# Windowed gated attention with a mixing layer behind it: maxima three patches ahead instead of four, residual tiles and mixed rows stored from ScalarE's queue

## The chip, the cores and the metric

One core of a Trainium2 chip runs the whole program. The metric is device time in microseconds of one execution, and the number that is compared is the median of several runs. A core has five engines with one in-order instruction queue each: TensorE (PE, with its weight loads as PEld), VectorE (DVE), ScalarE (ACT), GpSimd (POOL) and SyncE (SP). SP does no arithmetic here; it issues transfers between DRAM and the on-chip memory. Any instruction that waits for a semaphore holds everything behind it in its own queue.

## The reference

The input x is 8 batches of 512 rows and 2048 columns. Two layers are added to it. Both normalise each row first.

```python
x = x + tanh(g_x) * xattn(layernorm(x), ctx, mask)   # attention in windows
x = x + tanh(g_f) * ffn(layernorm(x))                # four streams, mixed

def xattn(qk, v, masks):            # 16 patches of 128 columns a batch
    q, k = Wq @ patches(qk) + bq, Wk @ patches(qk) + bk      # 256 x 128
    val = Wv @ patches(v) + bv
    scores = q_head.T @ k_head / sqrt(32)                    # 8 heads
    o = gelu(softmax(mask(scores)) @ val_head)
    return masks * (Wo @ o + bo)

def ffn(x):                         # x as 512 rows of 4 streams x 512
    xn = x * rsqrt(mean(x * x) + eps)
    H_res = sinkhorn(xn @ W_res.T + base, 50 iterations)     # 4 x 4 a row
    H_pre, H_post = softmax(xn @ W_pre.T + ..), softmax(xn @ W_post.T + ..)
    H = (1 - g) * I + g * H_res
    y = (H_pre-weighted sum of the streams) @ W_branch
    return H @ streams + H_post * y
```

## The kernel before

**Tiling.** A block is 512 columns (BLK), so a batch has 4 blocks and the run 32 blocks n, each of 4 patches t = 4n + p of 128 columns. A half is 256 columns, two patches. The main loop goes over patches, and in each step runs the letters of a string, ORDER, each of which emits one piece of work. Each piece has a priority. A scheduler then places the instructions in one order per engine, by priority and by its own picture of when their inputs are ready. So the order on the engines is not the order of the text, and a change of one piece moves many others.

**The attention's pieces.** `load_x` (L233) loads a block of x three blocks ahead, as two tiles `xt` of 128 x 2 x 512 numbers, from a pool of 10 such buffers. `proj(n)` normalises it, multiplies it in half-precision parts by the weights of q and k (L287 to L289), copies the result out of the accumulators as high and low halves (`ev`, L293 on ScalarE, L294 on VectorE), and SP stores these to DRAM (`qd`, L295). `stack(m)` loads one half back, rearranged by heads, into one of three buffers `QK` (L307, L312; L317 adds a mask row). A buffer is free again when `expo` of the half three before is done with it. `smax(t)` multiplies q by k for a patch (L345), VectorE takes the maxima (L348), TensorE transposes them (L353), ScalarE copies them (`mh`, L355), and SP stores them as rows 97 and 98 of the same QK buffer (L358). `expo(t)` multiplies again with these rows in (L632), so that the maxima are subtracted, and takes the exponential (L634). `attv` applies it to the values, which `vproj` made (L335, copied out at L336), and `outp(n)` applies gelu and mask, multiplies by Wo (L704 to L707), adds the result to x in place in the tile `xt` (L708, VectorE), sums squares of it for the next normalisation (`junk`, L710, ScalarE, which then reads the sum out), and stores the tile to a DRAM copy of the first layer's result, `x1s` (L711, SP). The four row tiles of a block are c = 0 to 3; c = 0, 1 are the two halves of one buffer, c = 2, 3 of the other.

The string has `P` (stacking) ahead of `s` (maxima) in one step. `AHEAD` says how many patches ahead of the current step the maxima are taken. With p = 2, `P` stacks the late half of the next block and `s` takes the maxima of patch t + AHEAD; with p = 3, `p` ends the projection of the block after next and stacks its first half.

**The mixing's pieces.** When a batch's attention is done, `ffn` computes its mixing matrices (the 50 Sinkhorn iterations are a long chain between GpSimd and VectorE, L881 to L891). Then each of its four row tiles is mixed from x1s, either by `mixv`, on VectorE, ScalarE and GpSimd (loads at L952, stores at L991), or by `mixp`, on TensorE: loads `xc` at L1008 into tiles of the xt pool, ScalarE at L1010, TensorE at L1011 (xpp), L942 to L944, L1045 and L1046 (mx), ScalarE at L1048 (`wp`), and a store by SP for each of four groups at L1049. `mixp` takes 12 of the 32 row tiles, all of batches 4 to 7, and nearly all of it runs after the attention is done.

Transfers signal their landing on eight semaphores that are used in turn, over both issuing queues. So a transfer also waits until the one before it on its semaphore has landed, unless another wait covers that.

Of the kernel before, what the change touches and what calls it, by code (L numbers as in the profile page):

```python
# [19 lines left out]
P = 128  # L20
# [5 lines left out]
BLK = 512  # L26
# [5 lines left out]
NS = 3  # L32
HI = 1000
XPRE_POOL = lambda b: b < 7
AHEAD = 4
LXP = 1
SK_POOL = lambda b: b < 7
CT_ACT = False
# [34 lines left out]
D_X1 = 0  # L73
# [24 lines left out]
def gated_xattn_mhc_kernel(  # L98
# [21 lines left out]
    V, A, G, T, SY = nc.vector, nc.scalar, nc.gpsimd, nc.tensor, nc.sync  # L120
# [82 lines left out]
    def defer(k, tag, fn):  # L203
        if k == 0:
            fn()
        else:
            late.append([k, fn, tag])
# [16 lines left out]
    x1s = {}  # L224
    G4 = {}
    ob = {}

    def load_x(n):
        b, k = divmod(n, NBLK)
        xtile[n] = []  # L230
        for c in (0, 2):
            t = xp_.tile([P, 2, BLK], F32, tag="xt", name="xt")
            SY.dma_start(t, x[b, c * P : (c + 2) * P, k * BLK : (k + 1) * BLK].rearrange("(c p) s -> p c s", p=P))  # L233
            xtile[n] += [t[:, 0], t[:, 1]]

    EXP_SET = "natural_log_exp_and_others"

# [124 lines left out]
    with tc.tile_pool(name="set", bufs=1) as st:  # L362
# [31 lines left out]
        for n in range(NBLK):  # L394
            load_x(n)
# [263 lines left out]
    def outp(n):  # L659

        b, k = divmod(n, NBLK)
        o = ob.pop(n)
        for g in range(2):
            gi = A.activation(o[:, g], o[:, g], AF.Gelu, bias=bvc[:, g : g + 1])  # L664
        with tc.issue_after(gi.ins), tc.high_priority():
            A.preload_act_table_set(EXP_SET)
        mb = gp.tile([P, BLK], F32, tag="mb", name="mb")
        SY.dma_start(mb, mask[b, k * BLK : (k + 1) * BLK].partition_broadcast(P))
        G.tensor_tensor(o, o, mb.unsqueeze(1).broadcast_to([P, 2, BLK]), ALU.mult)  # L669
        j0 = n * NP  # L670
        gt_ = op_.tile([P, NP, DK + 1], F32, tag="gT", name="gT")
        G.tensor_copy(gt_[:, :, DK], maskT[:, j0 : j0 + NP])
        yield
        for q in range(2):
            pt = ps_t.tile([P, 2, 2, P], F32, tag="t", name="gTp")
            for j in range(2):
                for e in range(2):
                    T.transpose(pt[:, j, e, :], o[:, e, (2 * q + j) * P : (2 * q + j + 1) * P], ident)
            V.tensor_copy(gt_[:, 2 * q : 2 * q + 2, 0:DK], pt.rearrange("p j e s -> p j (e s)"))
        g4 = ps_t.tile([P, DK + 1], F32, tag="t", name="g4")  # L680
        for p in range(NP):
            T.matmul(g4[32 * p : 32 * p + 32, :], Wm[:, k * NP + p, :], gt_[:, p, :], start=True, stop=True)
        if k == 0:
            g4s = lnp.tile([P, DK + 1], F32, tag="g4s", name="g4s", bufs=2)
            V.tensor_copy(g4s, g4)
            G4[b] = g4s
        else:
            V.tensor_tensor(G4[b], g4, G4[b], ALU.add)
        mr = MR[n % 2]
        SY.dma_start(mr[0:6, :], mrow_d[:, n * BLK : (n + 1) * BLK])  # L690
        gh = gp.tile([P, 2, BLK], F32R, tag="gh", name="gh")
        A.copy(gh, o)
        gl = gp.tile([P, 2, BLK], F32R, tag="gl", name="gl")
        G.tensor_tensor(gl, o, gh.bitcast(F32), ALU.subtract)
        if k == 0:
            sq2[b] = lnp.tile([P, 4, NBLK], F32, tag="sq2", name="sq2")
            x1s[b] = x1d.tile([D, S], F32, tag="x1s", name="x1s")
        xt = xtile.pop(n)
        yield
        for c in range(4):  # L700
            ps = ps_p.tile([P, BLK], F32, tag="p", name="op")
            cs = slice(c * P, (c + 1) * P)
            for e in range(2):
                T.matmul(ps, WoH[:, e, cs], gh[:, e], start=(e == 0), stop=False)  # L704
                T.matmul(ps, WoH[:, e, cs], gl[:, e], start=False, stop=False)  # L705
                T.matmul(ps, WoL[:, e, cs], gh[:, e], start=False, stop=False)
            T.matmul(ps, bo6[:, cs], mr, start=False, stop=True)  # L707
            V.tensor_tensor(xt[c], ps, xt[c], ALU.add)  # L708
            jk = fp.tile([P, BLK], BF16, tag="ph", name="junk2", bufs=BUF_PH)
            A.activation(jk, xt[c], AF.Square, bias=nmean[b][:, c : c + 1], accum_out=sq2[b][:, c, k : k + 1])  # L710
            defer(D_X1, "x1", lambda cs=cs, c=c: SY.dma_start(x1s[b][cs, k * BLK : (k + 1) * BLK], xt[c]))  # L711
            yield

    raws = {}
# [279 lines left out]
    def mixp(b, n, maps, inp=False):  # L994

        E, cst, pre, prc, post, rec, HR = maps
        rows = x1s[b].rearrange("d (j e) -> (d j) e", j=4)
        orow = out[b].rearrange("d (j e) -> (d j) e", j=4)
        PD = f1.tile([P, 4, 32], F32, tag="PD", name="PD", bufs=2)
        G.tensor_tensor(PD, blk.unsqueeze(1).broadcast_to([P, 4, 32]), rec[:, 4 * n : 4 * n + 4, 0:1].broadcast_to([P, 4, 32]), ALU.mult)  # L1000
        xc = []
        xo = xp_.tile([P, 2, 512], F32, tag="xt", name="xo")
        xps = (ps_t if inp else ps_p).tile([P, 512], F32, tag="t" if inp else "p", name="xpp")
        for g in range(4):
            q = 4 * n + g
            if g % 2 == 0:
                t2 = xp_.tile([P, 2, 512], F32, tag="xt", name="xc")
                SY.dma_start(t2, rows[q * P : (q + 2) * P, :].rearrange("(g p) s -> p g s", p=P))  # L1008
            t = t2[:, g % 2]
            A.activation(t, t, AF.Identity, bias=rec[:, q, 1:2])  # L1010
            T.matmul(xps[32 * g : 32 * g + 32, :], PD[:, g, :], t, start=True, stop=True)  # L1011
            xc.append(t)
        xs = xo[:, 0]
        A.copy(xs, xps)
        yield 1
        pt = (ps_t if inp else ps_p).tile([P, 4, P], F32, tag="t" if inp else "p", name="xpT")
        for e in range(4):
            T.transpose(pt[:, e, :], xs[:, e * P : (e + 1) * P], ident)
        y = ps_t.tile([P, 512], F32, tag="t", name="yp")
        if inp:  # L1020
            ph = fp.tile([P, 4, P], F16, tag="ph", name="ph", bufs=BUF_PH)
            pl = fp.tile([P, 4, P], F16, tag="pl", name="pl", bufs=BUF_PH)
        else:
            ph = xhp.tile([P, 4, P], F16, tag="xh", name="phb")
            pl = xhp.tile([P, 4, P], F16, tag="xl", name="plb")
        for r in branch(pt, ph, pl, y):
            yield r
        ys = xo[:, 1]
        A.copy(ys, y)
        yield 1  # L1030
        qh = xtp.tile([P, 2, 512], F32, tag="xTt", name="QD")
        QD = qh[:, 0].rearrange("p (t i) -> p t i", i=4)
        HD = qh[:, 1].rearrange("p (g t i) -> p g t i", g=4, i=4)
        G.tensor_tensor(QD, ident.unsqueeze(2).broadcast_to([P, P, 4]), post[:, n, :].unsqueeze(1).broadcast_to([P, P, 4]), ALU.mult)
        G.tensor_tensor(
            HD,
            blk.unsqueeze(1).unsqueeze(3).broadcast_to([P, 4, 32, 4]),
            HR[:, 4 * n : 4 * n + 4, :].unsqueeze(2).broadcast_to([P, 4, 32, 4]),
            ALU.mult,
        )  # L1040
        pw = None if inp else [ps_s.tile([P, 2, 512], F32, tag="s", name="mx") for _ in range(2)]
        for g in range(4):
            q = 4 * n + g
            ps = ps_t.tile([P, 512], F32, tag="t", name="mx1") if inp else pw[g // 2][:, g % 2]
            T.matmul(ps, QD[:, 32 * g : 32 * g + 32].rearrange("p t i -> p (t i)"), ys, start=True, stop=False)  # L1045
            T.matmul(ps, HD[:, g].rearrange("p t i -> p (t i)"), xc[g], start=False, stop=True)  # L1046
            w = fp.tile([P, 512], F32, tag="w", name="w", bufs=BUF_W) if inp else ep.tile([P, 512], F32, tag="eh" if g % 2 else "e32", name="wp", bufs=1 if g % 2 else BUF_EP)
            A.activation(w, ps, AF.Identity, bias=rec[:, q, 2:3])  # L1048
            SY.dma_start(orow[q * P : (q + 1) * P, :], w)  # L1049
            yield 1  # L1050

    NT_ = NTOT * NP
# [5 lines left out]

    for t in range(2, AHEAD):
        smax(t)  # L1060
    def at(name, fn, *args):

        p0 = tc.cur_priority
        tc.cur_priority = p0 + PRI[name]
        r = fn(*args)
        tc.cur_priority = p0 + tc.cur_priority - p0 - PRI[name]
        return r
# [15 lines left out]
    def act(c, t):  # L1083
# [20 lines left out]
        elif c == "l" and live_:  # L1104
            if p == LXP and n > 1 and n + 3 < NTOT:
                load_x(n + 3)
        elif c == "s" and live_ and t + AHEAD < NT_:
            at("smax", smax, t + AHEAD)
        elif c == "v" and live_:
# [119 lines left out]
```

## Time and profile before

| | us |
|---|---|
| three runs: median (lowest to highest) | 1695.94 (1693.8 to 1705.01) |
| profiled execution: time, span | 1699.8, 1698.0 |
| TensorE busy 141 to 567 / 567 to 992 / 992 to 1418 / 1513 to 1698 us | 398.1 of 426 / 377.9 of 425 / 357.9 of 426 / 160.5 of 185 |
| VectorE busy in the same | 242.2 / 331.9 / 332.2 / 123.1 |
| ScalarE busy in the same | 274.6 / 298.8 / 281.2 / 90.4 |
| DMA engines' mean busy share in the same | 0.77 / 0.71 / 0.63 / 0.46 |

The span runs from the first instruction to the last; the profiled execution's own time is 1.8 us longer. In this execution the mean granted TensorE clock is 0.954 of full speed. Up to about 141 us the weights are prepared and the first blocks projected; from 567 us on, attention and mixing of earlier batches run side by side; the last residual tile is stored at 1513 us, and from there to the end there is only the Sinkhorn chain of the last batches and mixing.

How to read it: a group line of the page names line, engine, operation, output and inputs with their shapes, and count; then busy time, mean duration in ns, and the idle time of the engine just before these instructions with what ended it. A line of waits says which engine stood before which line and for whom, in us in total, times, and the longest. SPq is SP's queue: it has no busy time, but its waits show what was held. The chain is the sequence of work that ended last, followed back from the end. The ends of matmuls are modelled, so a busy TensorE is not a TensorE at its peak.

Of the issues, the x1s stores are 128 of 256 KB and the mixed rows' stores (`wp`) 48 of 256 KB, all on SP; ScalarE issues nine small transfers in the first 15 us and none after.

### The profile page before, as it was taken

Reading aid. Unit: us, or ns where it says so; the run is one execution under the profiler, and the core shown is the slowest. Engines: PE = TensorE matmul, PEld = TensorE weight load, DVE = VectorE, ACT = ScalarE, POOL = GpSimd, SP = SyncE. Lnnn points to the kernel's source line nnn. Section 1 sums busy time; section 2 is a strip of 40 time slices with the busy share of each in tenths; the row PEclk is TensorE's granted clock in tenths of the full one; section 3 lists DMA queues with packets and bytes.
Section 4 is the critical chain, followed back from the end, with each engine's and each line's share of the span. In section 5 each row is a group of like instructions: output and inputs, shape, how many; then the busy total and the mean of one; then the engine's idle time right before and its main releaser. Section 6 shows DMA issues by size and latency. Waiting matters only on the chain.

```text
span 1698.0 us, 31628 instructions
## 1 busy us (share of the span) xinstructions
PE 1476.3 (87%) x10450; PEld 882.4 (52%) x10517; DVE 1190.8 (70%) x3552; ACT 1066.6 (63%) x1930; POOL 816.4 (48%) x1158
## 2 busy tenths in 40 slices
PE   4888989999998999889898878988888978789797
PEld 2445555665665655555455545555555545543233
DVE  7644434665686678877887687877976778867863
ACT  3347456667667666777578676686666656655354
POOL 1411413544554456556476665665656644643312
PEclk8899999999999999999999999999998989899899
DMA  5588886687578766876589666866566664335353
GB/s 188 154 251 247 254 252 182 185 258 224 166 213 243 219 190 190 257 245 182 155 271 286 181 181 183 243 211 181 160 188 180 191 167 114 129 120 151 107 168 119
DMA packets 257410, 330.53 MB, mean 195 GB/s; under 512 B 43543, under 2 KB 143191, under 8 KB 257246
## 3 DMA queue, kind: packets, MB, share of 16 engines
q1 hardware_dynamic: 255950, 328.18, 65.0%
q8 instruction: 83, 1.36, 0.3%
q14 instruction: 81, 0.66, 0.1%
q10 hardware_dynamic: 1296, 0.33, 0.1%
HBM read 226.71 MB, written 101.16 MB: 193 GB/s over the span
## 4 chain that ended last, share of the span: by engine, by line
PE 41%; DMA 22%; DVE 16%; ACT 9%; issue 6%; POOL 5%; SPq 1%; another core or an unknown queue 0%; POOLq 0%; ACTq 0%; DVEq 0%
PE vp L335 5%; DMA out_dram<-w 4%; DMA xs<-in_x_dram 3%; DMA QK<-qd 3%; DVE w L987 3%; PE qk L287 3%; PE qk L288 3%; PE qk L289 3%; DMA qd<-ev 3%; DMA xTt<-in_xT_dram 2%; PE op L704 2%; PE smax L345 2%; PE mx L1046 2%; PE mx L1045 2%; PE op L705 2%
## 5 line engine op out<-in xcount | busy, mean ns | idle before, releaser
L335 PE MATMUL vp<-Wv,ct 128*128 128x256 f32 x1024 | 255.9, 404 | 33.0 <-ACT VF L336 20.1
L335 PEld LDWEIGHTS vp<-Wv,ct 128*128 128x128 f32 x1024 | 203.5, 203 | 71.4 <-ACT VF L336 23.3
L887 POOL TENSOR_TENSOR W<-E,uv 128x64 f32<-128x64 f32 x343 | 111.7, 330 | 211.4 <-DVE uv L885 118.4
L348 DVE TENSOR_REDUCE smax<-smax 128x8 f32<-128x1024 f32 x128 | 155.7, 1217 | 75.6 <-PE smax L345 64.5
L275 POOL TENSOR_TENSOR xl<-xn,xh 128x512 f16<-128x512 f32 x126 | 157.6, 1251 | 106.4 <-ACT xh L273 100.3
L987 DVE SCALAR_TENSOR_TENSOR w<-x,Et,w 128x512 f32<-128x512 f32 x180 | 175.9, 978 | 45.2 <-POOL w L985 20.2
L287 PE MATMUL qk<-xh,WqkH 128*128 128x512 f16 x512 | 197.4, 386 | 7.2 <-DVE ev L294 4.5
L288 PE MATMUL qk<-xl,WqkH 128*128 128x512 f16 x512 | 197.2, 385 | 4.5 <-POOL xl L275 4.3
L289 PE MATMUL qk<-xh,WqkL 128*128 128x512 f16 x512 | 197.3, 385 | 0.0
L881 POOL TENSOR_TENSOR W<-E,uv 128x64 f32<-128x64 f32 x308 | 105.6, 348 | 183.8 <-DVE uv L891 81.7
L634 ACT ACTIVATE e<-sT,ebi,esc 128x1024 f32<-128x1024 f32 x128 | 153.2, 1197 | 42.1 <-PE sT L632 42.0
L704 PE MATMUL op<-gh,WoH 128*128 128x512 f32 x256 | 118.7, 465 | 28.6 <-DVE ev L294 20.6
L710 ACT ACTIVATE junk<-xt,nmean 128x512 bf16<-128x512 f32 x128 | 91.6, 716 | 82.0 <-DVE xt L708 37.7
L889 DVE TENSOR_REDUCE sm<-W 128x16 f32<-128x64 f32 x392 | 99.3, 256 | 56.2 <-POOL W L887 52.5
L270 POOL TENSOR_SCALAR xn<-xt,ln_r,nb 128x512 f32<-128x512 f32 x126 | 113.5, 901 | 40.6 <-DVE nb L254 25.0
L293 ACT ACTIVATE ev<-qk,bqs 128x512 f16<-128x512 f32 x128 | 86.4, 676 | 67.8 <-PE qk L289 64.7
L294 DVE SCALAR_TENSOR_TENSOR ev<-qk,bqs,ev 128x512 f16<-128x512 f32 x128 | 93.2, 729 | 47.4 <-ACT ev L293 46.9
L669 POOL TENSOR_TENSOR o<-o,mb 128x1024 f32<-128x1024 f32 x32 | 76.4, 2388 | 102.2 <-ACT o L664 102.2
L345 PE MATMUL smax<-QK 97*128 97x128 f16 x1024 | 83.9, 224 | 45.2 <-DMA QK<-qd 36.2
L883 DVE TENSOR_REDUCE sm<-W 128x16 f32<-128x64 f32 x352 | 72.8, 210 | 58.0 <-POOL W L881 54.1
L708 DVE TENSOR_TENSOR xt<-op,xt 128x512 f32<-128x512 f32 x128 | 86.8, 678 | 37.6 <-PE op L707 20.5
L985 POOL TENSOR_TENSOR w<-w,pj 128x512 f32<-128x512 f32 x60 | 79.6, 1327 | 64.1 <-ACT pj L984 32.6
(288 smaller groups left out, 3454.3 us busy)
## 6 DMA issues: line engine op xcount, KB each, us to landing
xt<-in_x_dram SPq DMA_DIRECT2D x64, 512.0 KB
ct<-in_cx_dram SPq DMA_DIRECT2D x64, 512.0 KB
qd<-ev SPq DMA_DIRECT2D x128, 256.0 KB
QK<-qd SPq DMA_DIRECT2D x64, 512.0 KB
xTt<-in_xT_dram SPq DMA_DIRECT2D x64, 512.0 KB
x1s<-xt SPq DMA_DIRECT2D x128, 256.0 KB
xs<-in_x_dram SPq DMA_DIRECT2D x56, 512.0 KB
x<-x1s SPq DMA_DIRECT2D x40, 512.0 KB
```

Of the source, the lines that this page charges most:

```text
L270: G.tensor_scalar(xn, xt[c], rstd1[b][:, c : c + 1], nb1[b][:, c : c + 1], ALU.mult, ALU.add)
L275: (V if n == 0 and c > 1 else G).tensor_tensor(l, xn, h, ALU.subtract)
L287: T.matmul(ps, WqkH[:, c, ms], hs[c], start=(c == 0), stop=False)
L288: T.matmul(ps, WqkH[:, c, ms], ls[c], start=False, stop=False)
L289: mm = T.matmul(ps, WqkL[:, c, ms], hs[c], start=False, stop=(c == 3))
L335: T.matmul(ps[:, h, :], ct[:, c, h * P : (h + 1) * P], Wv[:, c, :], start=(c == 0), stop=(c == 3))
L345: T.matmul(sc[:, h, :], q[0:97, h, sl], kk[0:97, h, sl], start=True, stop=True)
L348: V.tensor_reduce(mx, sc, AX.X, ALU.max)
L634: A.activation(e32, sc, AF.Exp, bias=ebi[:, t : t + 1], scale=esc[:, t : t + 1])
L704: T.matmul(ps, WoH[:, e, cs], gh[:, e], start=(e == 0), stop=False)
L887: (G if SK_POOL(b - B + 8) else V).tensor_tensor(W4[:, h], E4[:, h], ub[:, h], ALU.mult)
L987: V.scalar_tensor_tensor(w, x1[j], E[:, n, 4 * j + i : 4 * j + i + 1], w, ALU.mult, ALU.add)
```

## The change

Three edits. The maxima are taken three patches ahead instead of four. `load_x` remembers its two buffers in `xpair`, and `outp` stores a whole buffer, two row tiles in one transfer of 512 KB, from ScalarE's queue, after the Square of the second row tile in the text. `mixp` stores its rows from ScalarE's queue, after the ACTIVATE that writes them.

```diff
-AHEAD = 4
+AHEAD = 3
...
+    xpair = {}
...
             xtile[n] += [t[:, 0], t[:, 1]]
+            xpair[n, c // 2] = t
...
         xt = xtile.pop(n)
+        xb = [xpair.pop((n, i)) for i in range(2)]
...
             A.activation(jk, xt[c], AF.Square, bias=nmean[b][:, c : c + 1], accum_out=sq2[b][:, c, k : k + 1])
-            defer(D_X1, "x1", lambda cs=cs, c=c: SY.dma_start(x1s[b][cs, k * BLK : (k + 1) * BLK], xt[c]))
+            if c % 2:
+                A.dma_start(
+                    x1s[b][(c - 1) * P : (c + 1) * P, k * BLK : (k + 1) * BLK].rearrange("(c p) s -> p c s", p=P), xb[c // 2]
+                )
...
             A.activation(w, ps, AF.Identity, bias=rec[:, q, 2:3])
-            SY.dma_start(orow[q * P : (q + 1) * P, :], w)
+            A.dma_start(orow[q * P : (q + 1) * P, :], w)
```

`D_X1` is 0, so `defer` issued the old store at once. The maxima of patches 0 and 1 are taken before the loop in both kernels; the few in between, `range(2, AHEAD)`, are one fewer now.

## The prediction

> **What bounds the kernel now.** I read first the page's busy times and chain, then the waits of each engine, then single stretches of the timeline. The page:
>
> ```profile
> PE 1476.3 (87%) x10450; PEld 882.4 (52%) x10517; DVE 1190.8 (70%) x3552; ACT 1066.6 (63%) x1930; POOL 816.4 (48%) x1158
> ...
> PE 41%; DMA 22%; DVE 16%; ACT 9%; issue 6%; POOL 5%; SPq 1%; another core or an unknown queue 0%; POOLq 0%; ACTq 0%; DVEq 0%
> ```
>
> TensorE is busy most and has the largest share of the chain, but the second share is not an engine: it is the time in which the chain waits for a transfer. The chain's shares by line name QK<-qd and qd<-ev with 3% each, 102 us together. These are the two hops by which projected q and k go to DRAM and back as the heads lie in QK. The middle of the kernel (busy us of PE, PEld, DVE, ACT, POOL, then clock and DMA share):
>
> ```profile
> 567.00:992.00 425.00, 377.85 (x2872) 234.82 (x2895) 331.93 (x921) 298.78 (x542) 254.66 (x339) 0.98 0.71 212
> ```
>
> TensorE has 47 us of idle time in 425; VectorE is at 78%, ScalarE at 70%, the DMA engines at 71%. No engine is full: they hold one another up, and a stall that is removed is partly refilled by the next. Which stalls TensorE and SP's queue have (engine, line, what was waited for, us in total, times, longest):
>
> ```profile
> PE smax L345 <- DMA QK<-qd: 36.2, 18, 4.6
> PE op L704 <- DVE ev L294: 20.6, 14, 4.7
> PE vp L335 <- ACT VF L336: 20.1, 9, 8.5
> ```
> ```profile
> SPq L233 <- DMA x1s<-xt: 110.9, 42, 5.9
> SPq L1049 <- ACT wp L1048: 83.5, 38, 9.2
> ...
> SPq L711 <- DVE xt L708: 39.9, 26, 5.7
> ```
>
> TensorE's largest stall by far is the maxima's matmul at L345, for QK. SP's in-order queue is held at each x1s store until VectorE has added the tile (L711, with 27.1, 19.7, 17.1, 10.9 and 6.5 us more where another DVE instruction came last: 121 us), and at the next x load until a store has landed (L233). One such stall from hop to hop:
>
> ```profile
> 801.15 0.37 SPq L295 DMA_DIRECT2D qd<-ev  x1
> ...
> 806.14 0.64 SPq L307 DMA_DIRECT2D QK<-qd  x1
> 806.82 0.59 SPq L312 DMA_DIRECT2D QK<-qd  x1
> ```
> ```profile
> 813.79 0.61 PE L345 MATMUL smax<-QK 97*128 97x128 f16 x8 [3.05 <-DMA QK<-qd]
> ```
>
> From the store's issue to the load's 5.0 us, from there to the maxima 7.65 us: 12.6 us from a finished projection to usable heads. TensorE had less than that queued in between and stood 3.05 us.
>
> **Part 1, AHEAD 4 to 3.** A maximum is taken one patch later relative to the stacking that feeds it. In the built orders of the two kernels I counted TensorE's work between the two, at the durations of the profile (0.216 us from matmul to matmul of qk, 0.45 us for a patch's 8 smax matmuls, and so on). For a block's first patch (t = 4n), the median from the projection's last matmul to the smax goes from 10.8 to 15.4 us. For its third, the half that is stacked late because it must wait for expo of three halves before, the median from that expo to the smax goes from 11.4 to 21.0 us. With 12.6 us needed after a projection, and 7.65 us plus about 1.2 us for the two load issues after an expo, both medians now clear it; the lowest quarter of the first patches (12.5 us and less) does not. So of 36.2 us I take off a sixth as remaining: **-30 us**. Ends: 0, if the next wait (ev L294, VF L336) takes all of it, and -51 us, half of the chain's 102. I take a value near the row of waits, because it is a direct idle time of the engine with most of the chain. The price on the other side: the maxima have less time to come back as rows 97 and 98 before expo. From a maximum's transpose to its expo the median falls from 18.3–27.7 us (by patch) to 13.6–16.5 us of TensorE work; TensorE waits for these rows only 1.6 us now (sT for QK<-mh, once), and a patch takes some 11 us (the 1372 us from 141 to 1513 hold 124), so this costs nothing while the copy of mh and its store together stay under 13 us.
>
> **Part 2, x1s stores to ScalarE's queue, 128 to 64.** SP loses 128 issues of 0.34 us and its 121 us at L711. Who stands behind: qd and mh stores, QK loads. But these are hardly late: qd stores are issued a median 0.03 us after ev is written (67 us over all 128), and SPq has 1% of the chain. I book **-3 us**; ends -17 (that 1%) and +10: the pair now leaves after the second tile's add, and mostly after its Square (0.72 us and 0.19 for the sum's read-out), so it lands later and L233 is held longer than 2.6 us a time.
>
> ScalarE gets 64 issues. No ScalarE issue of this shape is in the trace; SP's load of the same shape (L233) takes 0.38 us, ScalarE's own at the start 0.34 to 0.93. 64 x 0.38 = 24.3 us. What of it is on the path: ScalarE holds 9% of the chain (153 us) with 1066.6 us of work, 14%. Queued behind each store are ev, VF, rc, e and mh, for which VectorE (46.9 us at ev) and TensorE (20.1 us at VF) wait. So **+3.5 us**; ends 0 (the issue runs while the Square does) and +24.
>
> The built order shows something that the code does not: of the 64 stores 41 stand directly behind both Squares, 8 between them and 15 ahead of both, up to 14 ScalarE instructions early. Those 23 wait in ScalarE's queue for the second tile's add, and hold what stands behind them. The nearest row is the Square's own wait for that add, 37.7 us in 32 times, 1.2 us each: 23 x 1.2 = 27 us of ScalarE, at 14% **+4 us**; ends 0 and +27.
>
> **Part 3, 48 mixed rows.** 48 x 0.33 us (L1049 on SP) = 16 us of issues on ScalarE; each also waits for its own ACTIVATE to end, which undoes the overlap of two in a row (1.27 us instead of 2 x 0.69): 0.11 x 48 = 5 us. 44 of them lie after 1525 us, where the chain is TensorE's xpp and mx, ScalarE is busy 49% of the time (90 of 185 us after 1513), and TensorE waits 1.6 us for wp. At 14%: **+3 us**; ends 0 and +21. The 83.5 us of SP at L1049 buy nothing: the xc load behind it waits for its buffer. At 1585.24 SP issues the store in 0.33 us, and the xc load goes only at 1586.23, when the mx matmul has let go of the tile.
>
> **What speaks against the move.** The trace counts 121 and 110.9 us of SP's waiting, and I book 3 us of it. The Trainium skill, DMA: Bandwidth & Descriptors, section "Issuing engines are not separate DMA queues", says that issuing from several engines saves only the sequencer's issue time; by it the SP term would be 0 and the sum 3 us higher. The Trainium skill, Perfetto Trace Analysis, section "DMA Instruction — HWDGE (DVE, Sync)", says that the descriptor generator is locked by one issuer at a time; by it a ScalarE issue can also wait out one of SP's, and no row here shows both queues at work in mid-kernel.
>
> **Sum.** From the profiled 1699.8 us (span 1698.0): -30 - 3 + 3.5 + 4 + 3 = -22.5, so 1677. The median of the runs shown, 1695.94, lies 3.9 us under the profiled run: **1674 us**.
>
> **Rivals.**
> - *The stall moves.* With QK in time, TensorE runs into ev L294 and VF L336 earlier; a quarter of the 36 us remains. 1699.8 - 9 + 10.5 = 1701, less 3.9: 1697. For it: VectorE at 78% and no engine full. Against: in 141 to 567 us, where VectorE is at 57%, 11.0 us of these stalls have no such neighbour.
> - *ScalarE's queue becomes the gate (slower).* Place: x1s stores in ScalarE's order; if an add or an earlier transfer is late, all of ev, VF, mh, e is late, so the loop through qd and QK is too. Price: 24.3 + 27 + 21 = 72 us of ScalarE, times the share f on the path, against 33 gained. It decides from f = 0.46; at f = 0.8 it is +25: 1721. For it: 23 stores ahead of their work. Against: 14% today.
> - *The loop is worth more than its stalls.* The two hops hold 102 us of the chain; half of it off and the costs as above: 1699.8 - 51 - 3 + 10.5 - 3.9 = 1652.
>
> **How the numbers follow.** Forecast 0.47, its own range 1658 to 1690, three quarters of it below 1679. Larger gain 0.12, moved stall 0.22, ScalarE the gate 0.19. About 1% (17 us) can be told from no change. Faster by more: 0.35 + 0.12 = 0.47; within: 0.12 + 0.22 = 0.34; slower: 0.19. Range: down to 1648, which leaves out the deep half of the larger gain (0.06), and up to 1714, which leaves out the upper two thirds of the gate (0.13).
>
> **What would show it.** In the waits of the changed kernel, L345 for QK<-qd under 10 us; at 30 or more part 1 failed. If the stall moved, ev and VF together grow past 60 us from 41. If ScalarE is the gate, its queue shows waits at the x1s store of over 50 us, and its chain share passes 14%. SP's waits at L233 well above 110.9 us, with qd stores late, would make part 2 a loss. The last stretch after the residual's last Square, 184 us now, should stay within 5 us. A tail 10 us longer would refute part 3.

## The result and the profile after

| | before | after |
|---|---|---|
| median of nine runs each on one chip (lowest to highest), us | 1698.72 (1693.8 to 1713.28) | 1713.25 (1709.3 to 1720.36) |
| profiled execution: time, span, us | 1699.8, 1698.0 | 1710.52, 1708.7 |
| mean granted TensorE clock | 0.954 | 0.945 |

The ratio is 1.0068, interval 1.0041 to 1.0095: slower, by less than 1%, where 1.3% faster was forecast. The page after, with busy times and the chain's shares by engine:

```profile
PE 1499.4 (88%) x10517; PEld 890.6 (52%) x10517; DVE 1199.2 (70%) x3552; ACT 1066.7 (62%) x1930; POOL 826.4 (48%) x1158
...
PE 43%; DMA 21%; DVE 16%; ACT 8%; issue 6%; POOL 5%; SPq 1%; ACTq 0%; POOLq 0%; DVEq 0%
```

ScalarE's share of the chain fell from 9% to 8%, and its queue (ACTq) has none: it did not become the gate. Now the waits of TensorE, after (engine, line, what was waited for, us in total, times, longest). The line numbers lie 2 to 7 higher than before: L348 is the old L345, L708 the old L704, L338 the old L335.

```profile
PE op L708 <- DVE ev L297: 19.4, 14, 3.7
PE gTp L681 <- POOL o L672: 17.0, 7, 6.6
PE g L685 <- DVE gT L682: 14.1, 10, 3.1
PE vp L338 <- ACT VF L339: 13.3, 8, 6.7
PE smax L348 <- ACT mh L358: 11.4, 8, 2.7
PE smax L348 <- DMA QK<-qd: 11.3, 4, 4.3
PE smax L348 <- ACT e L637: 10.8, 4, 3.2
```

Read as sums, this is what the prediction wanted. The wait for QK went from 36.2 to 11.3 us, and ev and VF together fell from 41 to 33 us. New are 22 us of waits at the maxima, for the accumulators that ScalarE has to read first (mh, e). The same stretch as before, by windows (busy us of PE, PEld, DVE, ACT, POOL, then clock, DMA share, GB/s):

```profile
567.00:992.00 425.00, 377.37 (x2819) 234.01 (x2812) 331.88 (x923) 291.54 (x530) 250.03 (x335) 0.95 0.71 211
```

TensorE is as busy as before (377.4 of 425 us, before 377.9) and did less: 2819 matmuls instead of 2872 (weight loads 2812 instead of 2895), at a clock of 0.95 instead of 0.98. So lost time does not all show as idle time; part of it is inside "busy". I counted the clock for itself: a mean clock of 0.954 over 1698.0 us is 78.1 us of clock not granted, 0.945 over 1708.7 us is 94.0. Summed from the single records of the clock, which the means round, it is 77.9 and 93.2: some 15 us more, in a span that grew by 10.7. TensorE was busy at half clock for 116 us before and for 151 us after.

How the clock is lost shows at one place, at the start of a batch's statistics. ScalarE after (start, us, operation, in brackets the idle time before it):

```profile
383.78 1.15 ACT L617 ACTIVATE xs<-xs,nmean 128x1024 f32<-128x1024 f32 x1 [3.79 <-DMA xs<-in_x_dram]
...
385.04 1.28 ACT L667 ACT_TABLE_LOAD   x1
386.34 1.33 ACT L667 ACTIVATE o<-o,bvc 128x512 f32<-128x512 f32 x2
387.69 1.28 ACT L669 ACT_TABLE_LOAD   x1
388.98 0.60 ACT L339 ACTIVATE VF<-vp 128x512 f32<-128x512 f32 x1
```

TensorE after, the first line that follows its matmuls of 382.59 us:

```profile
389.63 6.76 PE L338 MATMUL vp<-Wv,ct 128*128 128x256 f32 x16 [6.66 <-ACT VF L339]
```

And windows around it, after:

```profile
376.00:383.00 7.00, 6.97 (x40) 4.53 (x37) 3.97 (x14) 2.78 (x8) 2.57 (x7) 1.00 0.95 259
...
386.00:390.00 4.00, 0.37 (x1) 0.37 (x2) 0.00 (x0) 3.96 (x6) 2.25 (x1) 0.50 0.83 258
390.00:394.00 4.00, 4.00 (x10) 3.13 (x10) 1.83 (x7) 4.00 (x8) 1.24 (x5) 0.50 1.00 196
394.00:396.00 2.00, 2.00 (x6) 1.55 (x5) 0.56 (x2) 0.58 (x1) 1.34 (x1) 0.54 1.11 197
```

The square at L617 stands 3.79 us for its load. Behind it in ScalarE's order stand the activation o with its two table loads, and VF behind those. TensorE waits 6.66 us for VF. By the records of the clock it is at half from 385.6 to 395.8 us, so the first four of these ten microseconds fall into the wait, and the 16 vp matmuls behind it take 6.76 us. Before, at the same place, the last square ahead of the table loads (one further in the batch) waited less:

```profile
381.84 1.15 ACT L614 ACTIVATE xs<-xs,nmean 128x1024 f32<-128x1024 f32 x1 [1.37 <-DMA xs<-in_x_dram]
```

TensorE met two short waits instead of a long one (its two lines with idle time there, and the windows around them):

```profile
386.51 0.61 PE L345 MATMUL smax<-QK 97*128 97x128 f16 x8 [2.73 <-DMA QK<-qd]
...
388.40 5.41 PE L335 MATMUL vp<-Wv,ct 128*128 128x256 f32 x16 [0.84 <-ACT VF L336]
```
```profile
386.00:390.00 4.00, 2.66 (x20) 2.31 (x21) 2.57 (x6) 3.97 (x7) 2.61 (x2) 0.81 1.05 380
390.00:394.00 4.00, 4.00 (x18) 3.33 (x17) 1.11 (x5) 3.22 (x5) 2.44 (x3) 0.77 1.06 239
```

Before lost clock here too, but for 3.4 us (388.5 to 391.9) instead of 10.2. I read this place so: the wait for QK that the change removed held TensorE while ScalarE caught up. It is one place, and the order of TensorE's work differs there too (before, smax and sT stand ahead of vp).

### The profile page after: what moved, and what is told of

Read it like the earlier page. It is cut to its first block, busy times and chain, and to the rows that moved or that the text cites. A ratio compares the mean times of both kernels' runs of the same rounds, so it can differ in the third digit from the quotient of the medians.

```text
span 1708.7 us, 31497 instructions
## 1 busy us (share of the span) xinstructions
PE 1499.4 (88%) x10517; PEld 890.6 (52%) x10517; DVE 1199.2 (70%) x3552; ACT 1066.7 (62%) x1930; POOL 826.4 (48%) x1158
## 4 chain that ended last, share of the span: by engine, by line
PE 43%; DMA 21%; DVE 16%; ACT 8%; issue 6%; POOL 5%; SPq 1%; ACTq 0%; POOLq 0%; DVEq 0%
PE vp L338 5%; DMA out_dram<-w 4%; DMA qd<-ev 4%; DMA xs<-in_x_dram 3%; PE qk L290 3%; PE qk L291 3%; PE qk L292 3%; DVE w L994 3%; PE op L708 3%; DMA QK<-qd 2%; PE op L709 2%; PE mx L1052 2%; PE mx L1053 2%; PE op L710 2%; PE smax L348 2%
## 5 line engine op out<-in xcount | busy, mean ns | idle before, releaser
L338 PE MATMUL vp<-Wv,ct 128*128 128x256 f32 x1024 | 256.6, 403 | 28.4 <-ACT VF L339 13.3
L338 PEld LDWEIGHTS vp<-Wv,ct 128*128 128x128 f32 x1024 | 201.5, 202 | 64.7 <-issue 17.3
L273 POOL TENSOR_SCALAR xn<-xt,ln_r,nb 128x512 f32<-128x512 f32 x126 | 117.1, 929 | 68.1 <-DVE nb L257 55.3
L708 PE MATMUL op<-gh,WoH 128*128 128x512 f32 x256 | 120.4, 472 | 24.0 <-DVE ev L297 19.4
L297 DVE SCALAR_TENSOR_TENSOR ev<-qk,bqs,ev 128x512 f16<-128x512 f32 x128 | 93.4, 730 | 65.0 <-ACT ev L296 63.8
L348 PE MATMUL smax<-QK 97*128 97x128 f16 x1024 | 85.5, 226 | 35.4 <-ACT mh L358 11.4
L709 PE MATMUL op<-gl,WoH 128*128 128x512 f32 x256 | 107.4, 420 | 0.8 <-POOL gl L697 0.8
```

The source lines that it names most:

```text
L273: G.tensor_scalar(xn, xt[c], rstd1[b][:, c : c + 1], nb1[b][:, c : c + 1], ALU.mult, ALU.add)
L338: T.matmul(ps[:, h, :], ct[:, c, h * P : (h + 1) * P], Wv[:, c, :], start=(c == 0), stop=(c == 3))
L348: T.matmul(sc[:, h, :], q[0:97, h, sl], kk[0:97, h, sl], start=True, stop=True)
```

## The experiments

By adds I mean the last residual add of each block (L708 of before). Its time against before shows where a kernel falls behind; from the add of block 6 to that of block 19 before runs from 419 to 994 us. Ratios are against before on the same chip.

**The parts, one at a time.** Maxima three ahead alone:

```diff
-AHEAD = 4
+AHEAD = 3
```

> Only AHEAD 4 to 3; all stores stay on SP. Theory A (the stall moves: the maxima no longer wait for QK, but for the accumulators that mh and e still hold): within 5 us of before, 1694 to 1704, TensorE's waits at the smax for QK<-qd under 15 us, for ACT mh and ACT e together over 15 us. Theory B (ScalarE's queue is the gate and the loss comes from the x1s stores): the forecast's gain shows alone, 1672 to 1688. Theory C (the granted TensorE clock is what differs, 0.945 after against 0.954 before, because TensorE is asked for more in a shorter time): the mean clock is near 0.945 here too, and the time is 1700 to 1715 in spite of fewer waits.

Measured: 1732.86 us, ratio 1.0208 (1.0167 to 1.0249). The adds fall behind from +8 us at block 6 to +39 at block 19, and then hardly further (+42 at block 31). All three theories missed the time. QK's wait fell to 11.3 us and the waits at the maxima for mh and e rose to 26, as theory A has it, and the clock of 0.941 is as low as theory C has it, but the loss is about twice what C allowed.

The x1s stores alone, two by two from ScalarE's queue (the change's hunks at `load_x` and `outp`):

> Only the x1s stores move, in pairs, to ScalarE's queue; AHEAD stays 4, mixed rows stay on SP. Theory B: slower than before by 15 us or more, with waits at the x1s store in ScalarE's queue of over 50 us. Theory A: within 6 us of before. Theory C: the time follows the clock: near before if the clock is 0.954, 10 to 16 us slower if it is 0.945.

Measured: 1691.08 us, ratio 0.9951 (0.9927 to 0.9975). Theory B, a loss of 15 us or more, is refuted.

TensorE's mixed rows alone (the hunk at `mixp`):

> Only the 48 stores of the mixed rows move to ScalarE's queue. All theories: the stretch up to the last residual tile is as before; the tail of 185 us becomes 178 to 188 us (it is 180 us in the changed kernel, 5 us shorter), so 1691 to 1701. If the order of the attention phase comes out differently though its text is the same, up to 10 us either way show how much a new order alone moves.

Measured: 1697.85 us, ratio 0.9991 (0.9965 to 1.0017).

Both moves, maxima four ahead as before:

> Both moves of stores, AHEAD back at 4. Theory A: the moves cost about what the changed kernel lost, 1708 to 1718, since AHEAD is worth nothing. Theory B: slower than the changed kernel, 1725 or more, since the gain of AHEAD is missing. Theory C: the waits for QK<-qd return (30 us or more), the clock is near 0.954 and the time near before, 1694 to 1704.

Measured: 1689.85 us, ratio 0.9953 (0.9926 to 0.9981), faster than both kernels, and below what any of the theories had. The wait for QK is 28.2 us. What follows: the loss is the edit of AHEAD, all of it. The moves are a small gain, and the first of them carries it. Three ahead without the moves is worse by far (1.0208) than with them (1.0068).

**What three ahead breaks.** In three ahead alone ScalarE's wait for the statistics' loads is nearly three times that of before. The line of before, then that of three ahead:

```profile
ACT xs L614 <- DMA xs<-in_x_dram: 23.5, 18, 3.0
```
```profile
ACT xs L614 <- DMA xs<-in_x_dram: 63.8, 28, 7.1
```

In the trace two QK stacks lay 7 to 12 us apart before, mostly 8 to 10, with 28 to 50 us to the next pair; in three ahead alone mostly 1 to 8, with 31 to 53 to the next pair. The first load of a stack (L307) lands later (mean 7.65 us after issue instead of 6.80, the latest 13.8 instead of 10.4), and the latest of the statistics' loads at 12.0 us instead of 8.8. So I took the removed wait for a pacer, and tried that against a plainer theory, that a patch less between maxima and exponential is too little.

Spacing put back by hand, on SP's queue:

```diff
-            SY.dma_start(q[97:99, :, sl], mh)
+            last["mh"] = SY.dma_start(q[97:99, :, sl], mh)
...
-                at("stack", stack, NSB * (n + 1) + 1)
+                flush(lambda e: e[2] == "qd")
+                with tc.issue_after(last["mh"].ins):
+                    at("stack", stack, NSB * (n + 1) + 1)
```

> Maxima three ahead, nothing else of the change, and the late-half stack of each block held back on the sync engine's queue behind the store of the newest maxima rows, so that the two QK stacks of a block lie about 16 us of matrix work apart instead of 4 (before: 8). Pacing theory (the wait of TensorE for the first-half stack spaced the two stacks; without it they are issued together, the loads land late, and ScalarE stands in order at them with evictions behind it): ratio 1.000, between 0.993 and 1.008, and ScalarE's waits for DMA fall from 208 us towards the 152 of before. Margin theory (one patch less between a tile's maxima and its exponential, so TensorE waits for ScalarE's copy and exponentials, however the stacks lie): ratio stays at 1.016 to 1.026, and TensorE's waits in the maxima for the copied rows and the exponentials stay above 20 us.

Measured: 1714.53 us, ratio 1.0088 (1.0060 to 1.0116), between the ranges of the two theories. The stacks lay 16 to 36 us apart in the trace, their first loads landed in 6.16 us (mean), ScalarE's wait at the squares was 37.3 us, and its waits for transfers in all 167 us (152 before, 208 in three ahead alone). TensorE's waits at the maxima for mh and e fell to 15 us, which speaks against the margin theory. From block 6 to 19 the adds lose 19 us instead of 32. Over the whole run spacing alone gives back a bit over half.

Two ahead:

```diff
-AHEAD = 4
+AHEAD = 2
```

> Maxima two ahead, nothing else of the change. Pacing theory: the stacks are already together with three ahead (short spacing 4.4 us of matrix work there, 4.9 here), so nothing is left to lose: ratio 1.015 to 1.027, as with three. Margin theory: a second patch of margin is lost as the first was: ratio 1.035 to 1.05, and the waits of the maxima for the copied rows and the exponentials (26 us with three ahead) above 40 us.

Measured: 1742.8 us, ratio 1.0247 (1.0211 to 1.0282). The ratio lies where the pacing theory has it, but the trace shows another cause than in three ahead. ScalarE's wait at the squares is 34.9 us instead of 63.8, and TensorE's largest wait is now for the rows of the maxima:

```profile
PE sT L632 <- DMA QK<-mh: 49.5, 23, 6.9
```

It was 2.4 us in three ahead alone. So the margin between maxima and exponential is used up at two ahead, not yet at three, and this run supports neither theory as it was stated.

Four ahead for a block's first patch, three for the rest:

```diff
-            at("smax", smax, t + AHEAD)
+            for u in {0: (3, 4), 1: (), 2: (3,), 3: (3,)}[p]:
+                if t + u < NT_:
+                    at("smax", smax, t + u)
```

> Maxima three ahead for three patches of each block, four ahead for the first patch of a block alone (the one that waits for the first-half stack); nothing else of the change. Pacing theory: the wait that spaces the stacks is back, TensorE's waits for QK rise from 11 towards 36 us, and the ratio is 0.995 to 1.006. Margin theory: three of four patches still have the short distance, ratio 1.010 to 1.021.

Measured: 1695.91 us, ratio 0.9986 (0.9963 to 1.0008). The wait for QK is back and the loss is gone:

```profile
PE smax L345 <- DMA QK<-qd: 26.3, 13, 4.6
```

A third buffer for the statistics' loads, three ahead:

```diff
-BUF_XTP = 2
+BUF_XTP = 3
...
-        PD = f1.tile([P, 4, 32], F32, tag="PD", name="PD", bufs=2)
+        PD = f1.tile([P, 4, 32], F32, tag="PD", name="PD", bufs=1)
```

The text also takes each square one step later, which does nothing: without that the instructions of every engine come in the same order, because the scheduler places the square by its own picture of when the load has landed. `PD` with one buffer is to make room; by itself it leaves the orders of TensorE, ScalarE and SP as they were, though no run has it alone. The third buffer does reorder much: in the traces of three ahead without and with it, 1123 of the 1939 places in ScalarE's order hold another instruction.

> Maxima three ahead, and the squares of the statistics (on ScalarE) taken one step later behind their loads, with a third buffer for these loads (and, to make room, one buffer of the gated factors instead of two). Pacing theory: ScalarE's wait there falls from 63.8 us to below 20, and the time by most of that share of the loss: ratio 1.003 to 1.013 where three ahead alone has 1.021. Margin theory: the wait goes too, but ScalarE's idle time is no bound: ratio stays at 1.016 to 1.026.

Measured: 1696.6 us, ratio 0.9978 (0.9953 to 1.0003). More came back than the pacing theory asked for. The QK stacks are as close as without the buffer, and their first loads land as late (mean 7.58 us); what changed is the wait at the squares, which did not fall below 20 us as expected, but to 27.4:

```profile
ACT xs L615 <- DMA xs<-in_x_dram: 27.4, 14, 5.1
```

Part of the gain is another one: the adds are 14 us ahead by block 6 already.

The control, the same buffer with four ahead:

> Maxima four ahead as before, with the squares of the statistics one step later behind their loads, a third buffer for these and one buffer of the gated factors instead of two: the control of the run with three ahead and the same edit (ratio 0.998). Interaction theory (the edit heals what three ahead broke): here there is little to heal, ScalarE's wait at the squares was 23.5 us, so ratio 0.988 to 1.002, and three ahead is within 1% of four once the edit is in both. Additive theory (the edit is a gain of its own of some 2%, beside a loss of 2% that stays): ratio 0.972 to 0.984.

Measured: 1694.06 us, ratio 0.9956 (0.9921 to 0.9991). So with the buffer three ahead costs 0.2% more than four, which is within the noise; without it 2.1%. The additive theory is refuted: the two edits act on each other. But three ahead gains nothing here either, though TensorE's wait for QK is 7.0 us with it and 34.1 with four.

**The stand by itself.** The squares directly behind their own load in the text, four ahead:

```diff
-            if i > 0:
-                c, k = divmod(i - 1, 2)
-                A.activation(now, now, AF.Square, bias=nm[:, c : c + 1], accum_out=sq[:, c, k : k + 1])
+            if i < 8:
+                c, k = divmod(i, 2)
+                A.activation(xs, xs, AF.Square, bias=nm[:, c : c + 1], accum_out=sq[:, c, k : k + 1])
```

> Maxima four ahead, nothing of the change, but the squares of the statistics stand on ScalarE directly behind the issue of their own load instead of a step later, with the order of the stacks untouched: the suspected wait made large by itself. Theory that ScalarE's waits in order for loads stall TensorE: ScalarE's wait at the squares from 23.5 to 100 us or more, TensorE's waits for the eviction and for VF from 41 to over 80 us, more stalls of 3 us and over than the 3 of before in the blocks 6 to 20, mean clock below 0.945, ratio 1.02 to 1.08. Rival (ScalarE has slack, so its waits cost little): the wait grows, the ratio stays below 1.01.

Measured: 1701.84 us, ratio 1.0023 (0.9989 to 1.0057). It told nothing: the scheduler put nearly all squares where they had been (in the trace, 8 of the 1939 places in ScalarE's order hold another instruction than before), and the wait was as before:

```profile
ACT xs L614 <- DMA xs<-in_x_dram: 24.8, 18, 4.3
```

So the order was forced: the load behind the store of the newest maxima rows, the square at once, ScalarE's later work of the step behind the square.

```diff
+                with tc.issue_after(last["mh"].ins):
+                    SY.dma_start(xs.rearrange("p k s -> p (k s)"), x[b, c * P : (c + 1) * P, 2 * k * BLK : 2 * (k + 1) * BLK])
...
+                last["sq"] = A.activation(xs, xs, AF.Square, bias=nm[:, c : c + 1], accum_out=sq[:, c, k : k + 1])
...
         for c in ORDER:
-            act(c, t)
+            with tc.issue_after(last["sq"].ins) if last["sq"] is not None else ExitStack():
+                act(c, t)
```

> Maxima four ahead, nothing of the change. Each load for the statistics is issued behind the store of the newest maxima rows, its square follows at once, and ScalarE's further work of that step is queued behind the square: in the built order 0.3 us of matrix work (median) lies between a load's issue and its square, where before had 2.9. Theory that a stand of ScalarE at these loads stalls TensorE, and a stall of some 2.5 us halves the clock for 3 to 4 us more: ScalarE's wait at the squares from 23.5 to 120 us or more (56 squares, loads that land in 6 us), TensorE's waits for the eviction and for VF from 41 to over 70 us, clock lost between 340 and 1090 us from 19 us to over 35, ratio 1.020 to 1.070. Rival (ScalarE is idle a third of the span, so a stand costs little): the wait grows as much, the ratio stays below 1.010.

Measured: 1887.22 us, ratio 1.1106 (1.1079 to 1.1133). The waits of ScalarE and of TensorE in it:

```profile
ACT xs L615 <- DMA xs<-in_x_dram: 75.1, 25, 8.0
```
```profile
PE smax L345 <- DMA QK<-qd: 72.9, 23, 7.5
PE gTp L679 <- POOL o L670: 70.6, 14, 9.1
```

The size is above what either theory said, but the path is not the expected one. ScalarE's wait grew by 52 us, not by 100, and TensorE stood at QK and at o instead of at ev and VF. The forced order costs 188 us where the wait at the squares grew by 52, so it holds back more than the squares. That three ahead loses by the same path is not shown by it.

Its smaller dose, the same queueing with the square a step after its load, and the load where it was:

```diff
             if i > 0:
                 c, k = divmod(i - 1, 2)
-                A.activation(now, now, AF.Square, bias=nm[:, c : c + 1], accum_out=sq[:, c, k : k + 1])
+                last["sq"] = A.activation(now, now, AF.Square, bias=nm[:, c : c + 1], accum_out=sq[:, c, k : k + 1])
```

> The same queueing of ScalarE's work behind the square, but with the square a step later than its load, as before: 1.3 us of matrix work between the two (median) instead of 0.3. First theory: a smaller dose of the same, ratio between 1.003 and the other run's. Rival: within 1.010, no different from the other run.

Measured: 1712.71 us, ratio 1.0085 (1.0053 to 1.0117). The adds are 17 us late at block 0, 15 at block 6 and 22 at block 19: most of it is lost before the stretch in question, and the ratio fits both theories, so it decides nothing.

**Better kernels.** Both moves with the first patch alone four ahead:

> Both stores moved to ScalarE's queue as in the change, maxima four ahead for the first patch of a block and three for the others. If gains and losses add (moves 0.995, this order 0.999): ratio 0.990 to 0.998. If the moves only pay where the stacks lie as before: 0.998 to 1.010.

Measured: 1698.08 us, ratio 0.9994 (0.9962 to 1.0025): the moves add nothing to that order.

Both moves, four ahead, third buffer:

> Both stores moved as in the change, maxima four ahead, the squares one step later with a third buffer and one buffer of the gated factors. Candidate for the fastest: if the moves (0.995) and the later squares add, ratio 0.985 to 0.995; if the later squares give nothing where the maxima stay four ahead, 0.993 to 0.999.

Measured: 1688.9 us, ratio 0.9936 (0.9908 to 0.9965). This lies in both expected ranges.

The changed kernel itself with the third buffer:

> The changed kernel whole (maxima three ahead, both stores moved) with a third buffer for the statistics' loads, their squares a step later, and one buffer of the gated factors. If what three ahead costs is ScalarE's stand at these loads, the changed kernel mended there loses its 0.7%: ratio 0.990 to 1.000. If the third buffer only healed the kernel without the moves: 1.003 to 1.010.

Measured: 1671.9 us, ratio 0.9842 (0.9793 to 0.9892), the fastest of all, and below the range of 0.990 to 1.000 that the mending of three ahead was expected to give. Its waits for QK, and at vp for VF, and the stretch from 340 to 1090 us by windows:

```profile
PE smax L348 <- DMA QK<-qd: 11.9, 5, 4.4
...
PE vp L338 <- ACT VF L339: 6.4, 6, 1.6
```
```profile
340.00:1090.00 750.00, 687.46 (x5280) 427.74 (x5312) 578.86 (x1679) 524.64 (x965) 423.01 (x609) 0.98 0.74 219
```

The same stretch in three ahead alone:

```profile
340.00:1090.00 750.00, 663.71 (x4990) 416.91 (x5025) 547.62 (x1604) 490.23 (x900) 400.98 (x578) 0.95 0.72 203
```

The fastest kernel has 290 matmuls more in the same 750 us, at 0.98 of the clock instead of 0.95.

The same with two ahead:

> As the mended changed kernel (both stores moved, third buffer for the statistics' loads, one buffer of the gated factors), but maxima two ahead instead of three. If nothing of three ahead costs once the third buffer is in but QK stays late no longer, two ahead is the same within 0.5%: ratio 0.980 to 0.990. If the shorter distance to the exponentials has a price of its own, it shows here: 0.995 to 1.015.

Measured: 1700.34 us, ratio 0.9996 (0.9972 to 1.0020). Here the shorter distance has its own price, and names itself:

```profile
PE sT L636 <- DMA QK<-mh: 34.1, 21, 3.7
```

The ratios together:

| | four ahead | three ahead | three over four |
|---|---|---|---|
| nothing else | 1 | 1.0208 | 1.021 |
| third buffer | 0.9956 | 0.9978 | 1.002 |
| both moves | 0.9953 | 1.0068 (the change) | 1.012 |
| both moves and third buffer | 0.9936 | 0.9842 | 0.991 |

The third buffer takes 2.2% off three ahead with the moves and without them (0.9842 over 1.0068, 0.9978 over 1.0208), and 0.2 to 0.4% off four ahead. The moves take 1.4% off three ahead with and without the buffer, and 0.2 to 0.5% off four ahead.

And where the time is lost, in one profiled execution of each (340 to 1090 us; clock lost is the sum of what the granted clock lacks of 1, in windows of 1 us; single executions of before on one chip lie up to 28 us apart, 1684.6 to 1712.28, so single rows are rough):

| | TensorE stalls of 3 us and more: number, us | clock lost, us | adds, block 6 to 19, us |
|---|---|---|---|
| before | 3, 10 | 19 | 0 |
| three ahead alone | 8, 38 | 39 | +32 |
| after | 6, 24 | 32 | +15 |
| three ahead, spaced by hand | 5, 19 | 27 | +19 |
| two ahead | 6, 26 | 39 | +29 |
| three ahead, third buffer | 4, 17 | 27 | +7 |
| first patch four ahead | 2, 7 | 15 | +2 |
| both moves, four ahead | 3, 9 | 17 | -2 |
| after, third buffer | 0, 0 | 17 | -3 |
| four ahead, third buffer | 3, 11 | 17 | -5 |
| both moves, four ahead, third buffer | 5, 19 | 33 | +7 |
| both moves, first patch four ahead | 4, 16 | 26 | +12 |

The table does not rank the kernels. Both moves, four ahead, with the third buffer lost as much clock in its profiled execution as the changed kernel (33 and 32 us), and its ratio is 0.9936 where that has 1.0068.

## Why the prediction was wrong

**Part 1, the stall: right in kind.** L345 was to keep a sixth of its wait for QK and to lose 30 us. It kept nearly a third, 11.3 of 36.2 us (under 10 had been the mark), so 25 us of the wait went.

**Part 1, its price: the failed step.** The 30 us were booked as gain, one for one, "because it is a direct idle time of the engine with most of the chain", and the other side was priced only at the way from the maxima to expo: "so this costs nothing". That way did cost little: after, TensorE waits 1.9 us for QK<-mh, and only two ahead pays there (49.5 us alone, 34.1 with the moves and the third buffer). But the edit taken alone cost some 35 us (0.0208 of 1700) where 30 were to be gained. The runs put two things in the place of that step. First, the removed wait did work. It held TensorE by about 2 us at a time (36.2 us in 18 times; with a block's first patch alone four ahead it is back at 26.3). With it the QK stacks lie further apart; that ScalarE and the transfers catch up in it is read from one place of the trace. Putting it back for the first patch alone takes the loss away (0.9986); spacing the stacks alone takes a bit over half (1.0088); giving the statistics' loads a third buffer takes it away without bringing the wait back (0.9978, where four ahead has 0.9956). Second, the waits that came are fewer and longer, and a long stall is paid twice, once as idle time and once as clock: from before to three ahead alone, the stalls of 3 us and more grew from 10 to 38 us, and the clock lost from 19 to 39. A microsecond of removed wait was therefore not a microsecond of gain: even with the third buffer, where the loss is gone, three ahead has 27 us less wait for QK than four and is no faster (0.9978 and 0.9956).

**The forecast's rival "the stall moves"** named the right kind of effect and bounded it wrongly: it put the refill at ev and VF, with 60 us as its mark, and took no gain for the worst case. Ev and VF fell to 33 us. A sum of waits could not show the loss: the clock lost grew by some 15 us, and that is mostly inside TensorE's busy time (151 us busy at half clock instead of 116).

**Parts 2 and 3: mis-sized, part 2 with the wrong sign.** Booked at +4.5 and +3 us; measured 0.9951, about -8 us, and 0.9991, about -1.5 with an interval that holds 0. With three ahead the two are worth 24 us (1.0208 to 1.0068). SP's wait at the x load (L233, now L235) went from 110.9 to 94.9 us, where a loss was feared; it does not measure the gain either, since the fastest kernel has 110.2. SP's 121 us of waiting at L711 were in the profile, and I booked 3 of them, by SPq's 1% of the chain. Which transfer gains was not tried, nor whether the pairing or the move does it.

**The gate on ScalarE** is refuted: the chain's share is 8%, and the stores alone are faster. The 64 issues took 23.8 us of ScalarE's queue, as estimated. The list of ScalarE's waits has no lines for its issues, but the instructions next behind the 64 stores stood idle for 27 us in all, whatever ended it, where over 50 at the stores had been the mark. A ScalarE issue that waits out one of SP's, which the prediction held possible, does not show: in the changed kernel 35 of ScalarE's 112 issues behind the start overlap one of SP's in time, and the longest of all took 0.43 us where a pair's usual issue takes 0.37.

**The tail** behind the last Square went from 184 us to 178, a little more than the 5 us that the prediction allowed for, and to the good side. All 48 stores of the mixed rows lie after 1525 us, not 44, and the sum gives 1673 us, not 1674; neither matters.

**Luck.** The forecast of 1674 us is about what the changed kernel takes once the third buffer is in (1671.9 us). That is chance. Between both moves with the buffer at four ahead and at three, AHEAD is worth 0.9%, 16 us, not 30, and without the moves nothing; the rest comes from the buffer and the moves.

**What stays open.** Every edit lets the scheduler order all engines anew, so each run tests an edit and an order together. That three ahead collides with something at the statistics' loads is shown by the buffer, which takes 2.2% off both kernels with three ahead and 0.2 to 0.4% off those with four; whether it is ScalarE's in-order stand there, or an order that goes with it, is not shown. That late landings through close stacks make the stand long is shown only for about half, by the run spaced by hand; in the fastest kernel they land as late (mean 7.83 us). ScalarE's summed wait at the squares does not rank the kernels: the fastest has 32.6 us there, before 23.5.

## What to carry to other kernels

A wait that is removed may have been a pacer: ask which transfers it kept apart and which engine may have caught up in its shade, and look for the in-order stand that comes next before booking its time as gain. Read the clock beside the busy time: a stretch with the same busy share and fewer instructions has lost time that no list of waits holds, and here long stalls cost clock far more often than short ones. When an edit alone loses where it should have gained, run it together with a buffer more at the place it runs into, before it is given up: here it turned 1.0068 into 0.9842.

## What the hardware showed

TensorE's clock reacts to shorter stalls than I had thought. I took 340 to 1090 us of before, of three ahead alone, of both moves with four ahead, and of the first patch four ahead. A change to half clock came at most 3.4 us behind the gap's end after 26 of 28 gaps of 2.5 us and more between matmuls, after 7 of 9 between 2 and 2.5 us, after 7 of 31 between 1.5 and 2, and after 11 of 122 between 0.3 and 1.5. (The ends of matmuls are modelled, so a gap is known to a few tenths; one change can follow several gaps.) In every trace here the clock is either full or half, and changes only on a grid of 3.41 us: of the 40 stretches at half clock in the four, 28 lasted 3.41 us, 11 lasted 6.83 and one, behind a gap of 6.89 us, 10.24. So each step at half clock costs 1.7 us beside the stall itself, as far as TensorE has work in it. The Trainium skill, TensorE: Matmul & The Clock Gate, section "HAM oscillation — how this bites in real kernels", gives the rule as no idle gaps over some 3.4 us; here gaps well below that were followed by half clock, among them the 2.73 us before the smax at 386.51 us of before (with 0.84 us more behind it), so the measured bound is the one to plan by.
